# Expert layer of an eight-layer kernel: output product turned feature major, in float32r halves, with the token weights applied to the gated blocks

## The chip, the cores and the metric

The kernel runs on one core of one Trainium2 chip. The metric is the device time of one execution in microseconds, as the median of several runs. Profiles are of one execution; times in them are microseconds from the start of its span.

## The reference, cut to what matters

The program applies eight layers in a row to an activation of 2048 tokens with 128 features: attention and feed-forward layers in turn, each followed by a residual add and a layer norm. The change is in the fourth, a mixture of eight experts of which each token uses two:

```
gate_out = einsum('bsd,ed->bse', x, Wg)             # 8 logits per token
top_v, top_i = top_k(gate_out, 2)
probs = softmax(top_v)
for e in range(8):
    w_e = sum(probs * (top_i == e))                 # 0 for six of the eight
    h1 = einsum('bsd,hd->bsh', x, W1[e])            # 128 -> 256
    h2 = einsum('bsd,hd->bsh', x, W2[e])
    g = h1 * sigmoid(h1) * h2
    out = out + einsum('bsh,dh->bsd', g, W3[e]) * w_e
x = layernorm(x + out)
```

Every expert is computed for every token, and the weight (zero for most) is applied after.

## The kernel before, in words

The tokens lie in four batches of 512 (NB = 4), each as an SBUF tile X of 128 partitions by four chunks of 128 features. Eight stage classes run one after the other: Causal, F0, Rel, F1, Alibi, F2, A3, F3. F1 is the expert layer, lines 1939 to 2059.

The order of the work is written as Python generators that are stepped by hand: `K.step` (line 160) gives each generator of a list one turn, first the tails of the stage before; `K.tick` (line 148) gives one turn to the background list, which holds the set-up and the first batch of the *next* stage. A framework then places the instructions in each engine's queue by priority and by its own estimate of when operands are ready, and adds the semaphores. So each engine works strictly in order, but an instruction without open operands can stand far ahead of its place in the program. Tiles of one tag share a number of buffers (`bufs`); a new one waits until the oldest is free.

Float32 accuracy at float32r speed is had by halves: a value is split into a rounded part h and a rest l, and `mm3` (line 311) adds three products, wh·xh + wl·xh + wh·xl. `split_w` (line 290) loads a weight in chunks of 512 columns, casts h on VectorE and subtracts l on GpSimd.

In F1, `setup` (line 1949) loads and splits W1 and W2. `gate` (line 1969) works for one batch: it transposes X on TensorE (`xT`, line 317), copies X into the accumulator `acc` on GpSimd (line 1980), computes the logits (line 1984), ranks them on VectorE with a small GpSimd step (`rank`, line 1914), and leaves the weights `wt`, tokens on the partitions, in line 2000. `run` (line 2040) goes over batch b and expert e; each expert has two blocks of 128 hidden features (mm = 0, 1). `hidden` (line 2003) makes one block, hidden features on the partitions and 512 tokens along: six products of 512 columns into two PSUM banks, Silu on ScalarE (line 2012), and the product g of one bank with it on VectorE (line 2014). `out` (line 2017) follows one block later: for each of four chunks of tokens two float32 products with g as the stationary operand and W3 as the moving one (line 2025), which gives y with tokens on the partitions; then four scalar_tensor_tensor instructions on VectorE (line 2029) do acc = y · wt + acc. After the eighth expert the layer norm of `acc` writes X. The gate of the next batch is started at expert 2, and from the second batch on each block gives the next stage, Alibi, one background turn: its set-up, its first batch, and the maxima of scores (lines 695 and 697).

Of the kernel before, what the change touches and what calls it, by code (L numbers as in the profile page):

```python
# [7 lines left out]
F32 = mybir.dt.float32  # L8
F32R = mybir.dt.float32r
# [3 lines left out]
ALU = mybir.AluOpType  # L13
# [3 lines left out]
P = 128  # L17
NB = 4
T = 512
# [20 lines left out]
class K:  # L40
# [115 lines left out]
    def next(self):  # L156
        self.uid += 1
        return self.uid
# [131 lines left out]
    def split_w(self, pool, src, n, name, scales=(), tag=None, raw=("wraw", 1)):  # L290

        nc = self.nc
        h = pool.tile([P, n], F32R, name=name + "h", tag=(tag or name) + "h")
        l = pool.tile([P, n], F32R, name=name + "l", tag=(tag or name) + "l")

        def fill():
            for s in range(0, n, 512):
                e = min(n, s + 512)
                w = pool.tile([P, 512], F32, tag=raw[0], name=f"wraw{self.next()}", bufs=raw[1])
                self.late(nc.sync.dma_start(w[:, :e - s], src[:, s:e]))  # L300
                yield
                yield
                for a, b, f in scales:
                    if a <= s < b:
                        nc.vector.tensor_scalar(w[:, :e - s], w[:, :e - s], f, None, ALU.mult)
                nc.vector.tensor_copy(h[:, s:e], w[:, :e - s])
                nc.gpsimd.tensor_tensor(l[:, s:e], w[:, :e - s], h[:, s:e].bitcast(F32), ALU.subtract)
                yield
        return h, l, fill()

    def mm3(self, out, wh, wl, xh, xl):
        nc = self.nc
# [142 lines left out]
class Attn:  # L455
# [4 lines left out]
    nb, lead, lag, ahead = 3, 8, 5, 2  # L460
    span, keep = "last", True
# [167 lines left out]
class Causal(Attn):  # L629


    alibi, nm = False, "a0"

    def weights(self):
        k, d, pool = self.k, self.k.d, self.early
        h, l, fill = k.split_w(pool, d["a0_w"], 256, "a0wqk")
        next(fill)
        bqk = k.load(pool, d["a0_b"][0:256].rearrange("(a p) -> p a", p=P), [P, 2], "a0bqk")
        self.pads(0)
        wv = k.load(pool, d["a0_w"][:, 256:384], [P, P], "a0wv")  # L640
        bv = k.bcast(pool, d["a0_b"][256:384], P, "a0bv")
        wo = k.load(pool, d["a0_wo"], [P, P], "a0wo")
        bo = k.bcast(pool, d["a0_bo"], P, "a0bo")
        self.w = dict(qkh=h, qkl=l, v=wv, o=wo, bqk=bqk, bv=bv, bo=bo)
        yield from fill
# [57 lines left out]
    def rows_out(self, t, mx):  # L703
        k, nc, pool = self.k, self.nc, self.wk
        yield
        yield
        yield from k.turn(True)
        ps = k.bank("b")
        for c in range(4):
            k.tr(ps[:4, c * P:(c + 1) * P], mx[:, c, :])  # L710
        yield
        nm = pool.tile([4, T], F32R, tag="nm", name=f"nm{t}", bufs=2)
        nc.scalar.activation(nm, ps[:4, :], AF.Copy, scale=-1.0)
        self.mrow(t, nm)
        self.rows_at = t
        yield
# [82 lines left out]
class Alibi(Causal):  # L799
    MROW, alibi, nm = 30, True, "a2"  # L800
    nb, lead, pre, span = 4, 12, True, "first"
# [18 lines left out]
class Rel(Attn):  # L820
# [3 lines left out]
    R, MROW, NV, nm = 64, 48, 2, "a1"  # L824
    nb, lead, lag, ahead = 3, 6, 4, 3
# [302 lines left out]
class A3:  # L1128


    nm, span, keep, la = "a3", "last", True, 2
# [377 lines left out]
class F0:  # L1509


    nm, span, keep = "f0", "first", True
# [426 lines left out]
class F1:  # L1939


    nm, span, keep = "f1", None, True
    banks = dict(s=4, o=2, b=2)

    def __init__(self, k):
        self.k, self.nc = k, k.nc
        self.x, self.wt, self.acc = {}, {}, {}

    def setup(self):
        k, d, pool = self.k, self.k.d, self.early  # L1950
# [18 lines left out]
    def gate(self, b, X):  # L1969

        k, nc, w = self.k, self.nc, self.w
        u = k.next()
        pool = self.pool if b else self.early
        self.x[b] = yield from k.xT(pool, X, full=True, bufs=2 if b else 1)
        xf = self.x[b][2]
        if b == 0:
            acc = self.acc[b] = pool.tile([P, 4, P], F32, name="acc0")
        else:
            acc = self.acc[b] = k.sh.tile([P, 4, P], F32, tag="ot", name=f"acc{u}", bufs=2)
        nc.gpsimd.tensor_copy(acc, X)  # L1980
        yield from k.turn()
        ps = k.bank()
        for c in range(4):
            nc.tensor.matmul(ps[:, 8 * c:8 * c + 8], xf[:, c * P:(c + 1) * P], w["g"], start=True, stop=True)
        yield
        lg = pool.tile([P, 4, 8], F32, tag="lg", name=f"lg{u}", bufs=2)
        nc.vector.tensor_copy(lg, ps[:, :32].rearrange("p (c e) -> p c e", e=8))
        m = pool.tile([P, 4], F32, tag="m", name=f"m{u}", bufs=2)
        ex = pool.tile([P, 4, 8], F32, tag="ex", name=f"ex{u}", bufs=2)
        wt = self.early.tile([P, 4, 8], F32, tag="wt", name=f"wt{u}", bufs=2)  # L1990
        nc.vector.tensor_reduce(m, lg, AX.X, ALU.max)
        nc.vector.tensor_tensor(ex, lg, m[:, :, None].to_broadcast([P, 4, 8]), ALU.subtract)
        nc.scalar.activation(ex, ex, AF.Exp)
        yield
        rk = yield from rank(k, pool, lg, w["tri"], 8, 4, f"f1{u}")
        nc.vector.tensor_scalar(rk, rk, 1.5, None, ALU.is_lt)
        nc.vector.tensor_tensor(ex, ex, rk, ALU.mult)
        nc.vector.tensor_reduce(m, ex, AX.X, ALU.add)
        nc.vector.reciprocal(m, m)
        nc.vector.tensor_tensor(wt, ex, m[:, :, None].to_broadcast([P, 4, 8]), ALU.mult)  # L2000
        self.wt[b] = wt

    def hidden(self, b, e, mm):
        k, nc, w, pool = self.k, self.nc, self.w, self.pool
        xh, xl, _ = self.x[b]
        s = [k.bank("s") for _ in range(2)]
        for j in range(2):
            ws = slice(512 * e + 256 * j + P * mm, 512 * e + 256 * j + P * mm + P)
            k.mm3(s[j], w["1h"][:, ws], w["1l"][:, ws], xh, xl)
        u = k.next()  # L2010
        sl = pool.tile([P, T], F32, tag="sl", name=f"sl{u}", bufs=3)
        nc.scalar.activation(sl, s[0], AF.Silu)  # L2012
        g = pool.tile([P, T], F32, tag="g", name=f"g{u}", bufs=5)
        nc.vector.tensor_tensor(g, s[1], sl, ALU.mult)
        return g

    def out(self, b, e, gs, X):
        k, nc, w = self.k, self.nc, self.w
        acc = self.acc[b]
        while b not in self.wt:  # L2020
            yield
        y = k.bank("o")
        for c in range(4):
            for mm in range(2):
                nc.tensor.matmul(y[:, c * P:(c + 1) * P], gs[mm][:, c * P:(c + 1) * P], w["3"][:, 2 * e + mm, :],  # L2025
                                 start=(mm == 0), stop=(mm == 1))
        yield
        for c in range(4):
            nc.vector.scalar_tensor_tensor(acc[:, c, :], y[:, c * P:(c + 1) * P], self.wt[b][:, c, e:e + 1], acc[:, c, :],
                                           ALU.mult, ALU.add)  # L2030
        yield
        if e == 7:
            yield
            if b == NB - 1:
                k.layernorm(acc, X)
            else:
                yield from k.norm(acc, X)
            k.finish(self, b, X)

    def run(self, Xs):  # L2040
        k = self.k
        self.w["3"] = k.load(self.pool, k.d["f1_w3"], [P, 16, P], "f1w3")
        gs = []
        last = None
        for i in range(8 * NB + 1):
            b, e = divmod(i, 8)
            if e == 2 and b + 1 < NB:
                gs.append(self.gate(b + 1, Xs[b + 1]))
            g = []
            for mm in range(2):  # L2050
                if i < 8 * NB:
                    g.append(self.hidden(b, e, mm))
                if mm == 0 and last:
                    gs.insert(0, self.out(*last))
                k.step(gs)
                if b:
                    k.tick()
            last = (b, e, g, Xs[min(b, NB - 1)])
        k.leave(self, gs, 0)


class F2:
    nm, span, keep = "f2", None, False
# [116 lines left out]
class F3:  # L2180


    nm, span, keep = "f3", None, True
    lag, ahead, steps = 4, 7, 2
# [97 lines left out]
    def weigh(self, b, j, h):  # L2282
        k, nc, w = self.k, self.nc, self.w
        while b not in self.cT:
            k.step(self.gs)
        cb = k.bank("t")
        nc.tensor.matmul(cb, w["sel"][:, j, :], self.cT[b], start=True, stop=True)
        nc.vector.tensor_tensor(h, h, cb, ALU.mult)
# [119 lines left out]
```

## Time and profile before

| | us |
|---|---|
| median of 3 runs | 2244.88 (2244.24 to 2246.5) |
| the profiled execution, its time | 2239.62 |
| its span | 2237.9 |
| TensorE busy (matmuls) | 2025.4, 91% of the span |
| VectorE busy | 1664.1, 74% |
| ScalarE busy | 1333.5, 60% |
| GpSimd busy | 501.9, 22% |
| F1's output matmuls (line 2025), first to last start | 1053.9 to 1209.1 |
| F1's accumulation (line 2029), 128 instructions | 37.8 |

In the profile PE is TensorE's matmuls, PEld its weight loads, DVE is VectorE, ACT is ScalarE, POOL is GpSimd, SP the engine that issues most DMAs. An instruction is named by its line, its operation, what it writes and what it reads (`o<-f1w,g`), and its shapes. A row of a group gives its busy time, the mean duration in ns, and the idle time of the engine just before it with what ended that. Busy time of an engine is not work on the path: what a change in one stage is worth is read from that stage, and there from what ends last.

### The profile page before, as it was taken

The numbers are of one execution on the slowest core, as the hardware profiler recorded it, in microseconds if no ns is written. First come the engines' busy times: TensorE is split into PE (matmuls) and PEld (weight loads), VectorE is DVE, ScalarE is ACT, GpSimd is POOL, SyncE is SP. The second block draws the span as 40 slices with busy tenths as digits, with TensorE's granted clock in tenths as the row PEclk, the third lists the DMA queues.
The fourth block names the chain that finished last, engine by engine and source line by source line (L and its number), as shares of the span: only waits on it lengthen the run. The fifth ranks groups of instructions, "written<-read, shape, count | busy, mean of one in ns | idle before, by whom it ended". The sixth has DMA issues, their size and how long they took to land.

```text
span 2237.9 us, 43122 instructions
## 1 busy us (share of the span) xinstructions
PE 2025.4 (91%) x14400; PEld 1477.7 (66%) x14400; DVE 1664.1 (74%) x5592; ACT 1333.5 (60%) x2983; POOL 501.9 (22%) x706
## 2 busy tenths in 40 slices
PE   7999788888888999999999999998999999999897
PEld 4666566676665667676887665786666566666676
DVE  5778689888878677873777785544777877778787
ACT  3566787787734656665333666333777777767632
POOL 3222212111212532433000322531111111111220
PEclk9999999999978999999999999999999999999999
DMA  5321322021433454421021420604888878888400
GB/s 171 106 77 35 109 50 57 6 48 27 116 113 108 130 175 125 127 65 57 15 67 48 116 78 15 219 17 112 214 209 198 211 192 193 199 194 211 99 5 15
DMA packets 264918, 242.10 MB, mean 108 GB/s; under 512 B 106352, under 2 KB 190618, under 8 KB 263866
## 3 DMA queue, kind: packets, MB, share of 16 engines
q1 hardware_dynamic: 259146, 221.33, 37.2%
q0 software_dynamic: 5232, 17.50, 3.3%
q8 instruction: 115, 1.88, 0.3%
q14 instruction: 105, 0.86, 0.1%
q10 hardware_dynamic: 320, 0.52, 0.1%
HBM read 103.82 MB, written 74.32 MB: 80 GB/s over the span
## 4 chain that ended last, share of the span: by engine, by line
PE 59%; DVE 17%; ACT 10%; DMA 7%; issue 4%; POOL 2%; SPq 1%; ACTq 0%; POOLq 0%; DVEq 0%
PE t L219 5%; PE s L2129 4%; PE o L1393 3%; PE o L744 3%; PE s L695 3%; PE t L728 3%; PE o L1032 3%; PE b L313 3%; PE b L219 3%; PE o L2025 3%; DMA a3dpw<-p 2%; PE s L313 2%; PE b L315 2%; PE b L314 2%; PE s L315 2%
## 5 line engine op out<-in xcount | busy, mean ns | idle before, releaser
L985 DVE CUSTOM_DVE_ANT_0 junk<-w,a1mask 128x640 bf16<-128x640 f32 x256 | 203.1, 818 | 67.3 <-PE w L983 65.4
L219 PE MATMUL t<-ident,p 128*128 128x128 f32 x1280 | 201.9, 279 | 23.8 <-ACT p L1350 15.7
L772 ACT ACTIVATE Pt<-t 128x384 f32<-128x384 f32 (+1 forms) x384 | 179.5, 528 | 65.8 <-PE t L728 54.4
L219 PEld LDWEIGHTS t<-ident,p 128*128 128x128 f32 x1280 | 151.7, 142 | 81.0 <-ACT p L1350 39.0
L1363 ACT COPY PT<-t 128x512 f32<-128x512 f32 x256 | 149.9, 596 | 71.9 <-PE t L219 70.9
L1059 ACT ACTIVATE Pt<-t 128x512 f32<-128x512 f32 x256 | 149.1, 597 | 72.7 <-PE t L1058 44.5
L1350 ACT ACTIVATE p<-s,nb 128x512 f32<-128x512 f32 x256 | 178.6, 702 | 12.8 <-DVE nb L1349 8.4
L1349 DVE TENSOR_REDUCE nb<-s 128x1 f32<-128x512 f32 x256 | 175.0, 687 | 2.6
L1368 DVE CUSTOM_DVE_ANT_0 jk<-p,a3right 128x496 bf16<-128x496 f32 (+3 forms) x256 | 125.0, 488 | 29.2 <-ACT p L1350 17.8
L697 DVE CUSTOM_DVE_ANT_0 junk<-s,a0mask 128x128 bf16<-128x128 f32 (+3 forms) x256 | 114.2, 485 | 43.4 <-PE s L695 42.4
L697 DVE CUSTOM_DVE_ANT_0 junk<-s,a2mask 128x128 bf16<-128x128 f32 (+3 forms) x256 | 114.9, 484 | 28.3 <-PE s L695 27.9
L781 POOL TENSOR_SCALAR_AFFINE_SELECT Pt<-Pt 128x512 f32<-128x512 f32 x112 | 69.9, 636 | 249.0 <-ACT Pt L772 248.9
L1344 PE MATMUL s<-a3KT,a3QT 128*128 128x512 f32 x256 | 118.9, 465 | 7.3 <-DMA a3K<-L 4.1
L1347 DVE TENSOR_TENSOR s<-s,W 128x160 f32<-128x160 f32 (+1 forms) x256 | 81.1, 318 | 56.1 <-PE s L1345 55.2
L1393 PE MATMUL o<-PT,V 128*64 128x512 f32 x512 | 116.9, 599 | 0.5 <-ACT PT L1363 0.5
L1707 ACT ACTIVATE p<-sm,nb 128x128 f32<-128x128 f32 x256 | 100.6, 396 | 24.8 <-DVE nb L1705 24.3
L1345 PE MATMUL s<-a3K,a3Q 128*128 128x512 f32 x256 | 102.7, 401 | 0.1
L1705 DVE CUSTOM_DVE_ANT_0 sm<-s,band,rn 128x128 f32<-128x128 f32 x256 | 78.3, 344 | 26.5 <-PE s L1692 19.3
L1056 PE MATMUL t<-a1Q,a1K 128*128 128x512 f32 (+3 forms) x256 | 92.4, 366 | 6.2 <-ACT Pt L1059 3.6
L695 PE MATMUL s<-a0K,a0Q 128*128 128x256 f32 (+2 forms) x256 | 83.6, 387 | 14.0 <-DVE mx L697 6.8
L982 PE MATMUL w<-a1K,a1Q 128*128 128x256 f32 (+2 forms) x192 | 83.8, 437 | 9.3 <-DVE mx L985 8.3
L2012 ACT ACTIVATE sl<-s 128x512 f32<-128x512 f32 x64 | 38.0, 598 | 91.0 <-PE s L315 85.6
(494 smaller groups left out, 5812.7 us busy)
## 6 DMA issues: line engine op xcount, KB each, us to landing
W<-a3dsk SPq DMA_DIRECT2D x32, 640.0 KB
a1Q<-a1iq SPq DMA_DIRECT2D x32, 512.0 KB
a3dpw<-p SPq DMA_DIRECT2D x64, 160.0 KB
a3dpw<-p SPq DMA_DIRECT2D x64, 144.0 KB
a1K<-a1ik SPq DMA_DIRECT2D x64, 128.0 KB
a3Q<-a3dim SPq DMA_DIRECT2D x32, 256.0 KB
a3KT<-H POOLq DMA_DIRECT2D x64, 128.0 KB, 4.4
a3KT<-H SPq DMA_DIRECT2D x64, 128.0 KB
```

The lines of the kernel that those rows point to most:

```text
L219: return self.nc.tensor.matmul(out.bitcast(x.dtype), x, i[:n, :n], is_transpose=True, start=start, stop=stop)
L695: self.scored = nc.tensor.matmul(s[:, :nm], self.qof(0, t, i)[:, qc * P:(qc + 1) * P], Ks[:, i, :nm], start=True, stop=True).ins
L697: nc.vector.tensor_tensor_reduce(junk[:, :n], s[:, :n], k.mask[:, 512 - n:512], 1.0, NEG, ALU.add, ALU.max, mx[:, qc, i:i + 1])
L772: ready = nc.scalar.activation(Pt[:, i, z:], s[:, z:], AF.Exp, scale=sc).ins
L985: nc.vector.tensor_tensor_reduce(junk, s.rearrange("p a n -> p (a n)")[:, T - n:T + m], k.mask[:, T - n:T + m], 1.0, NEG, ALU.add, ALU.max ...
L1059: nc.scalar.activation(Pt[:, i, :T], s, AF.Exp, scale=sc)
L1344: nc.tensor.matmul(s, QT[:, e, qs], KT[:, e, :], start=True, stop=False)
L1349: nc.vector.tensor_reduce(nb, s, AX.X, ALU.min)
L1350: nc.scalar.activation(p[:, e, :], s, AF.Exp, bias=nb, scale=-1.0, accum_out=den[:, qc, 2 * un + e:2 * un + e + 1])
L1363: self.copied[t] = nc.scalar.copy(PT[e][:, :, qc * P:qc * P + P], tb.rearrange("p (c n) -> p c n", n=P)).ins
L1368: nc.vector.tensor_tensor_reduce(jk[:, :nn], p[:, e, x0:], w["right"][:, :nn], 1.0, 0.0, ALU.mult, ALU.add, at[:, e, qc, 31:32])
L1393: m = nc.tensor.matmul(o[64 * e:64 * e + 64, :], V[:, kc, h * 64:h * 64 + 64], PT[e][:, kc, :], start=(kc == 0), stop=False)
```

## The change

Only F1 and one helper are touched. W3 is now split into halves by `split_w` in the stage itself (its raw chunks use the buffers of the Silu outputs) and is the stationary operand; the gated block is the moving one. Each block of 128 hidden features gives three float32r products of 512 columns, and the 48 products of a batch accumulate in one PSUM bank, with output features on the partitions. The weights can then no longer be a scalar per partition. They are applied before: `gate` transposes them to 8 rows of 512 tokens, writes the rows to DRAM, and `weights` reads each row back, spread over all 128 partitions, as a 512-column tile `cb` (four buffers). `weigh` multiplies g by it on GpSimd, in place, copies the rounded half on ScalarE and subtracts the other on VectorE. `weigh` is called two blocks after `hidden`, `out` two after that. At the end of a batch the result is copied to SBUF, transposed back, and X is added on VectorE; the accumulator in SBUF, its copy of X and the 128 accumulations are gone. The cut diff:

```diff
+    def rows_out(self, rows, name):
+        n = rows.shape[0]
+        d = self.dr.tile([n, T], F32, tag=f"rows{n}", name=name, bufs=2)
+        self.nc.gpsimd.dma_start(d, rows)
+        return d
...
-    nm, span, keep = "f1", None, True
+    nm, span, keep, lag = "f1", None, True, 2
...
-        nc.gpsimd.tensor_copy(acc, X)
...
         nc.vector.tensor_tensor(wt, ex, m[:, :, None].to_broadcast([P, 4, 8]), ALU.mult)
-        self.wt[b] = wt
+        yield
+        yield from k.turn()
+        ps = k.bank()
+        for c in range(4):
+            k.tr(ps[:8, c * P:(c + 1) * P], wt[:, c, :])
+        yield
+        wr = pool.tile([8, T], F32, tag="wr", name=f"wr{u}", bufs=1)
+        nc.scalar.copy(wr, ps[:8, :])
+        self.rows[b] = k.rows_out(wr, f"f1rows{b}")
+        if b:
+            yield from self.weights(b)
+
+    def weights(self, b):
+        cb = self.wt[b] = []
+        for i in range(8):
+            cb.append(self.pool.tile([P, T], F32, tag="cb", name=f"cb{b}{i}", bufs=4))
+            self.nc.gpsimd.dma_start(cb[i], self.rows[b][i].partition_broadcast(P))
+            for _ in range(0 if b == 0 and i < 2 else 2):
+                yield
...
-        sl = pool.tile([P, T], F32, tag="sl", name=f"sl{u}", bufs=3)
+        sl = pool.tile([P, T], F32, tag="sl", name=f"sl{u}", bufs=2)
...
-        g = pool.tile([P, T], F32, tag="g", name=f"g{u}", bufs=5)
+        g = pool.tile([P, T], F32, tag="g", name=f"g{u}", bufs=self.lag + 1)
...
+    def weigh(self, b, e, g):
+        nc.gpsimd.tensor_tensor(g, g, self.wt[b][e], ALU.mult)
+        h, l = (pool.tile([P, T], F32R, tag="g" + x, name=f"g{x}{u}", bufs=3) for x in "hl")
+        nc.scalar.copy(h, g)
+        nc.vector.tensor_tensor(l, g, h.bitcast(F32), ALU.subtract)
+        return h, l
...
-        y = k.bank("o")
-        for c in range(4):
-            for mm in range(2):
-                nc.tensor.matmul(y[:, c * P:(c + 1) * P], gs[mm][:, c * P:(c + 1) * P], w["3"][:, 2 * e + mm, :],
-                                 start=(mm == 0), stop=(mm == 1))
-        yield
-        for c in range(4):
-            nc.vector.scalar_tensor_tensor(acc[:, c, :], y[:, c * P:(c + 1) * P], self.wt[b][:, c, e:e + 1], acc[:, c, :],
-                                           ALU.mult, ALU.add)
...
+        if i == 0:
+            self.acc[b] = k.bank("o")
+        y, (h, l) = self.acc[b], g
+        for n, (p, q) in enumerate(((w["3h"], h), (w["3l"], h), (w["3h"], l))):
+            nc.tensor.matmul(y, p[:, i * P:(i + 1) * P], q, start=(i == n == 0), stop=(i == 15 and n == 2))
+        if i < 15:
+            return
+        yield
+        yT = k.sh.tile([P, T], F32, tag="os", name=f"yT{b}", bufs=1)
+        nc.scalar.copy(yT, y)
+        yield
+        yield from k.turn()
+        ps = k.bank("b")
+        for c in range(4):
+            k.tr(ps[:, c * P:(c + 1) * P], yT[:, c * P:(c + 1) * P])
+        yield
+        r = k.sh.tile([P, 4, P], F32, tag="ot", name=f"r{b}", bufs=2)
+        nc.vector.tensor_tensor(r, ps.rearrange("p (c n) -> p c n", c=4), X, ALU.add)
...
-        self.w["3"] = k.load(self.pool, k.d["f1_w3"], [P, 16, P], "f1w3")
...
+        h, l, fill = k.split_w(self.pool, k.d["f1_w3"].rearrange("p a n -> p (a n)"), 2048, "f1w3", raw=("sl", 2))
+        self.w["3h"], self.w["3l"] = h, l
+        while 0 not in self.rows:
+            k.step(k.bg)
+        gs, q, r = [self.weights(0), fill], [], []
+        n, lag = 16 * NB, self.lag
+        for i in range(n + lag + 2):
+            b, j = divmod(i, 16)
+            if j == 2 and b + 1 < NB:
+                gs.append(self.gate(b + 1, Xs[b + 1]))
+            if i < n:
+                q.append(self.hidden(b, j // 2, j % 2))
+            if lag <= i < n + lag:
+                b, j = divmod(i - lag, 16)
+                while b not in self.wt or len(self.wt[b]) <= j // 2:
+                    k.step(gs)
+                r.append(self.weigh(b, j // 2, q[i - lag]))
+            if i >= lag + 2:
+                b, j = divmod(i - lag - 2, 16)
+                gs.insert(0, self.out(b, j, r[i - lag - 2], Xs[b]))
+            k.step(gs)
+            if i >= 16:
+                k.tick()
```

More of the change, by code (lines that the diff above doesn't have):

```diff
@@ L1946, in __init__ @@
         self.k, self.nc = k, k.nc
-        self.x, self.wt, self.acc = {}, {}, {}
+        self.x, self.wt, self.acc, self.rows = {}, {}, {}, {}
     def setup(self):
@@ L1975, in gate @@
         xf = self.x[b][2]
[L1976 to L1979, printed above, removed]
-        nc.gpsimd.tensor_copy(acc, X)
         yield from k.turn()
@@ L2010, in hidden @@
         u = k.next()
-        sl = pool.tile([P, T], F32, tag="sl", name=f"sl{u}", bufs=3)
+        sl = pool.tile([P, T], F32, tag="sl", name=f"sl{u}", bufs=2)
         nc.scalar.activation(sl, s[0], AF.Silu)
-        g = pool.tile([P, T], F32, tag="g", name=f"g{u}", bufs=5)
+        g = pool.tile([P, T], F32, tag="g", name=f"g{u}", bufs=self.lag + 1)
         nc.vector.tensor_tensor(g, s[1], sl, ALU.mult)
         return g
-    def out(self, b, e, gs, X):
-        k, nc, w = self.k, self.nc, self.w
-        acc = self.acc[b]
-        while b not in self.wt:
-            yield
-        y = k.bank("o")
+    def weigh(self, b, e, g):
+        k, nc, pool = self.k, self.nc, self.pool
+        u = k.next()
+        nc.gpsimd.tensor_tensor(g, g, self.wt[b][e], ALU.mult)
[3 more added lines that the diff above has]
+        return h, l
@@ new lines, in out @@
+    def out(self, b, i, g, X):
+        k, nc, w = self.k, self.nc, self.w
+        if i == 0:
[11 more added lines that the diff above has]
+        ps = k.bank("b")
@@ L2031, in out @@
+        nc.vector.tensor_tensor(r, ps.rearrange("p (c n) -> p c n", c=4), X, ALU.add)
         yield
[L2032 to L2038, printed above, removed]
+        if b == NB - 1:
+            k.layernorm(r, X)
+        else:
+            yield from k.norm(r, X)
+        k.finish(self, b, X)
     def run(self, Xs):
         k = self.k
-        self.w["3"] = k.load(self.pool, k.d["f1_w3"], [P, 16, P], "f1w3")
@@ L2043, in run @@
[L2043 to L2047, printed above, removed]
-                gs.append(self.gate(b + 1, Xs[b + 1]))
[L2049 to L2058, printed above, removed]
+        h, l, fill = k.split_w(self.pool, k.d["f1_w3"].rearrange("p a n -> p (a n)"), 2048, "f1w3", raw=("sl", 2))
```

## Prediction

> **What bounds the kernel now.** I read the page's chain first: TensorE ends last for 59% of the span and VectorE for 17%, and the old output matmuls (line 2025) are one of its lines, at 3%. That says where to look, not what a change there is worth, so I then cut the expert stage F1 into 20 us stretches. It fills 1050 to 1210 us.
>
> ```profile
> core 0: us, PE busy (x) PEld busy (x) DVE busy (x) ACT busy (x) POOL busy (x), PEclk, DMA share, GB/s
> 1070.00:1090.00 20.00, 20.00 (x121) 17.28 (x120) 13.29 (x42) 8.11 (x13) 1.29 (x4) 1.00 0.00 0
> 1150.00:1170.00 20.00, 20.00 (x122) 17.39 (x121) 15.49 (x51) 7.74 (x12) 1.85 (x5) 1.00 0.00 1
> 1190.00:1210.00 20.00, 20.00 (x131) 17.70 (x130) 12.28 (x39) 4.55 (x8) 0.00 (x0) 1.00 0.00 1
> sum 160.00, PE 158.18 PEld 138.84 DVE 118.01 ACT 52.98 POOL 15.23; mean PE 19.77 PEld 17.36 DVE 14.75 ACT 6.62 POOL 1.90
> ```
>
> TensorE has no gap at full clock; VectorE is busy 118.0 of 160 us, ScalarE 53.0, GpSimd 15.2. TensorE's order of work sets this stage. Third, the timeline of one expert (columns: start, duration, engine, line, operation), for the spacing of instructions, since a matmul's own duration overlaps its neighbours':
>
> ```profile
> 1130.40 0.40 PE L314 MATMUL s<-xTh,f1wl 128*128 128x512 f32 x1
> 1130.64 0.39 PE L315 MATMUL s<-xTl,f1wh 128*128 128x512 f32 x1
> 1130.87 1.95 PE L2025 MATMUL o<-f1w,g 128*128 128x128 f32 x16
> 1132.57 0.48 PE L313 MATMUL s<-xTh,f1wh 128*128 128x512 f32 x1
> 1132.85 1.13 DVE L2029 SCALAR_TENSOR_TENSOR acc<-o,wt,acc 128x128 f32<-128x128 f32 x4 [1.02 <-PE o L2025]
> 1132.89 0.40 PE L314 MATMUL s<-xTh,f1wl 128*128 128x512 f32 x1
> ```
>
> A 512-column float32r matmul starts 0.233 us after the one before. The eight float32 output matmuls of an expert run as 16 and take 1130.87 to 1132.66 (1132.89 less one spacing), 1.79 us; the chain has them at 1.78.
>
> **The change, part by part.**
>
> TensorE. Per expert the 1.79 us become 2 blocks x 3 products x 0.233 = 1.40 us, so 32 x 0.39 = 12.5 us go. Seven sets of four transposes come into the stage (weights of three batches; the result of four). A set in this stage takes about 0.45 us to the next matmul's start (1112.76 to 1113.11, plus that matmul's slow start), so 3.2 us. Net -9.3 us: **TensorE alone would need 150.7 us for the stretch.** The set for batch 0 lies in Rel, some 130 us ahead of its use (line 2000 runs at 915 us).
>
> ScalarE. 64 copies of the weighted block at 0.61 us (row of line 930) are 39 us, plus seven evacuations at 0.58: 53 + 43 = 96 us of 160, hidden under TensorE; a table reload is not to be expected, since copies already stand between the Silus today.
>
> VectorE. 32 groups of four scalar_tensor_tensors at 1.13 us go: -36.2. Added are 64 subtractions 128x512 at 0.64 (0.69 alone, 0.60 when the next follows at once): +41.0; four casts of W3 at 0.42 (line 306): +1.7; four adds of X at 0.69: +2.8. Sum 118.0 + 9.3 = 127.3 us. By the sum that still fits under 150.7.
>
> GpSimd. The two copies of X in the stretch go (-1.2). Added are 64 multiplications 128x512, which have a direct row elsewhere (line 1649), four subtractions for W3 of the same kind, and 32 broadcasts and 3 row writes, each an issue like line 1312's. That is 15.2 - 1.2 + 68 x 1.28 + 35 x 0.52 = 119 us. A broadcast also has to wait, on GpSimd's own queue, until its rows have landed in DRAM; landing takes 4.4 us (median of line 1312's issues), three times in the stretch: 132 us. Behind that wait stand the next multiplications, and for them ScalarE's copies. They have the two iterations of lag, some 4.5 us, as cover; a wait longer than that would stop TensorE.
>
> ```profile
> L1649 POOL TENSOR_TENSOR kr<-kr,tb 128x512 f32<-128x512 f32 x32 | 40.9, 1278 | 171.3 <-DVE kr L1641 136.6 <-DVE rs L351 8.4 <-DVE rs L344 6.5
> L1312 POOL DMA_DIRECT2D a3KT<-H x64 | 33.4, 524 | 173.1 <-ACT H L1307 153.6 <-ACT bd L1270 19.5
> L930 ACT CAST r0h<-t 128x512 fp32r<-128x512 f32 x4 | 2.5, 616 | 1.8 <-POOL t L925 1.8
> ```
>
> So each engine alone fits. **The cost is where GpSimd and VectorE meet.** Three pairs from the timelines of other stages:
>
> ```profile
> 1477.54 0.29 DVE L366 BATCH_NORM_STATS2 lnst<-r 128x6 f32<-128x128 f32 x1
> 1477.54 1.29 POOL L2092 TENSOR_TENSOR hhl<-h,hhh 128x512 fp32r<-128x512 f32 x1 [4.30 <-DVE hhh L2091]
> ...
> 1483.30 1.30 POOL L2092 TENSOR_TENSOR hhl<-h,hhh 128x512 fp32r<-128x512 f32 x1 [0.43 <-DVE rs L346]
> 1483.32 1.29 DVE L347 TENSOR_TENSOR rs<-rs,lnv 128x4 f32<-128x4 f32 x1
> ...
> 349.48 1.28 POOL L1649 TENSOR_TENSOR kr<-kr,tb 128x512 f32<-128x512 f32 x1 [3.98 <-DVE kr L1641]
> 349.92 1.46 DVE L1639 TENSOR_TENSOR tb<-ta,tab 128x256 f32<-128x256 f32 x2
> ```
>
> In the first, a VectorE instruction with one SBUF input runs beside GpSimd's at its usual 0.29. In the second, a tiny one with two SBUF inputs (median 0.155) takes 1.29 and ends with GpSimd's. In the third, two large ones with two SBUF inputs (about 0.76 for the pair) take 1.46. The stage today has next to none of this, because GpSimd is nearly idle and both 128x512 operands of line 2014 are not in SBUF. The new subtraction reads g and h, both in SBUF; the new multiplication runs 64 times. The two exclude each other.
>
> What a subtraction waits: from nothing (it always slips in ahead) to 1.28 us (always behind a whole multiplication). I take the middle in two ways. Multiplications fill 82 of 160 us, so a random arrival waits 0.51 x 0.64 = 0.33 us. Laid out by hand at TensorE's pace (block product in VectorE, then multiplication, copy, subtraction), the waits alternate between 0 and about 0.8, mean 0.41. So 64 x 0.33 to 0.41 = 21 to 26 us. The small two-input instructions of four layer norms and three gates (some 15 each, 105 in all) come in runs, of which I let a third wait 0.33: 11 us. VectorE then needs 127.3 + 24 + 11 = 162 us, more than TensorE's 150.7, and in an order that waits for ScalarE and TensorE as well; 4 us for that gives **166 us in place of 160, +6 us**. The outer ends are 150.7 (no wait) and 127.3 + 64 x 1.28 = 209 us.
>
> A rule that speaks against the new DMAs on GpSimd: line 1312's 64 issues, the nearest row, span only 0.516 to 0.551 us, so the sum above takes 0.52. The Trainium skill, "SBUF — State Buffer", section "SBUF: two separate sides", says that a DMA issued by GpSimd starves while VectorE runs a two-port copy, some 620 ns alone becoming 3100. An estimate from that page, for the four W3 casts alone, would be 4 x 2.5 = 10 us more on GpSimd; the trace of before shows no such case, and the sum goes by the row.
>
> Ends of the stage. At its start W3 (1 MB, one DMA now) comes in four chunks through the buffers of Silu; the first output block is now due two iterations later, after about 1056 us, and chunk and broadcast, issued near 1048.5, should land by 1053: nothing, or 2 us if a broadcast is late. At its end the result passes one copy, four transposes and an add before the norm, some 3 us later; Alibi's first matmuls cover batch 3, and batch 0's, four to five steps later, push about one unit of Alibi's maxima (0.6 us) past the stage. I count +1 and -1 (four copies of X and the DVE stalls behind Alibi's memsets today) as nothing.
>
> **Rivals.** (1) TensorE keeps setting the pace: if the subtractions mostly run right after the block product, before the multiplication has started, they wait little; spare VectorE time is 150.7 - 127.3 = 23 us, that is 0.36 us per subtraction. For: it stands right behind the block product in VectorE's queue, while the multiplication must first be told that the product is done. Against: its own copy from ScalarE must be done by then. It gives -9 us, 2235 to 2236 (by the median). This is the case on the other side; it decides when the mean wait is under 0.2 us, with 64 x 0.2 + 11 = 24. (2) GpSimd becomes the bound: its 132 us plus 64 waits behind subtractions of up to 0.6 (38 us) are 170, and bunched in the batches that also hold Alibi's four memsets (1.8 us each) and the W3 split; 175 to 190 us, +15 to +30. For: a queue that also waits for DMAs. Against: batch 3 has none of that. (3) The gains and waits cancel, -4 to +2.
>
> **How the numbers follow.** The sum is made against the profiled execution, 2239.6 us (span 2237.9). Runs shown have a median of 2244.9, 5.3 above, so I add 5.3: 2239.6 + 6 + 5.3 = 2251 us. Chances: forecast (+2 to +14) 0.42; TensorE bound (-4 to -11) 0.27; GpSimd bound 0.18; cancelled 0.13. A measurement of this kernel can tell about 0.2%, 4.5 us. Of the forecast's 0.42 about 0.09 lies under that, so faster 0.27, same 0.22, slower 0.51. The range 2235 to 2273 reaches from TensorE's bound to nearly the end of GpSimd's case. Cases of both signs hold much; the forecast's own range is 2247 to 2259.
>
> **What would show it.** Right: in 1050 to 1210, subtractions with a mean above 0.9 us ending together with multiplications, TensorE idle for VectorE or waiting for the halves at the output matmuls, GpSimd near 80% busy. TensorE's step is right if an expert's six output matmuls take 1.40. Rival 1 shows in subtractions of 0.69 and TensorE at 20.00 in every stretch. Rival 2 shows in ScalarE waiting for GpSimd, and GpSimd for row DMAs. Wrong in kind: a different order of instructions after the stage, or Alibi starting late.

## The result and the profile after

The changed kernel takes 2271.55 us (median of 5 runs, 2268.40 to 2277.44) against 2244.88 before: ratio 1.0126, interval 1.0104 to 1.0148. It is slower, as forecast, but by 26.7 us and not by 6. The profiled execution took 2273.53 us (span 2271.7).

The stage is now read from F1's first Silu to its last: 155.5 us before (1050.5 to 1206.0), 184.2 after (1056.2 to 1240.4). These 28.7 us are most of the 33.8 by which the two profiled spans differ; the first Silu itself comes 5.7 us later. The share of the chain that ended last has moved from TensorE to VectorE and to waits (page of the kernel after, shares of the span; before, TensorE had 59% and VectorE 17%):

```profile
PE 53%; DVE 20%; ACT 10%; DMA 6%; issue 6%; POOL 3%; SPq 1%; ACTq 0%; POOLq 0%; DVEq 0%
```

The stretches of the kernel after (columns as in the table of the prediction; three parts of the stage, then the whole):

```profile
core 0: us, PE busy (x) PEld busy (x) DVE busy (x) ACT busy (x) POOL busy (x), PEclk, DMA share, GB/s
1062.00:1086.00 24.00, 15.38 (x62) 11.07 (x61) 23.68 (x51) 10.29 (x17) 19.82 (x16) 0.94 0.49 164
1110.00:1134.00 24.00, 23.33 (x107) 18.18 (x105) 20.17 (x48) 14.76 (x26) 17.96 (x18) 1.00 0.23 73
1160.00:1185.00 25.00, 19.89 (x74) 15.74 (x72) 16.94 (x53) 11.14 (x18) 10.92 (x13) 0.80 0.45 133
1056.00:1246.00 190.00, 160.52 (x676) 119.77 (x675) 160.83 (x326) 90.31 (x156) 130.22 (x121) 0.96 0.28 85
```

TensorE was idle 1.8 of 160 us before (busy 158.18 in the sum of the prediction's table) and is now idle for 29.5 of 190. The last row holds the surprise of this case: VectorE is busy 160.8 us (forecast 162), GpSimd 130.2 (forecast 132). The loads came out as worked out, and yet the stage takes 190 us and not 166. The groups that answer to the rows of the prediction (kernel after, 1056 to 1246):

```profile
L2042 POOL TENSOR_TENSOR g<-g,cb 128x512 f32<-128x512 f32 x64 | 90.7, 1424 | 48.2 <-DVE g L2035 34.1 <-DMA cb<-f1rows 2.5 <-DVE rs L358 2.0
L2045 DVE TENSOR_TENSOR gl<-g,gh 128x512 fp32r<-128x512 f32 x64 | 68.3, 1067 | 20.2 <-ACT gh L2044 19.9
L356 DVE TENSOR_SCALAR rs<-rs 128x4 f32<-128x4 f32 x4 | 4.8, 1191 | 0.0
```

GpSimd's multiplication takes 1424 ns (1278 where it was looked up), the subtraction 1067 (0.64 to 0.69 us by itself), and an instruction on 128x4 elements 1191 ns. The same instruction before (lines of the kernel before, 1049 to 1210):

```profile
L349 DVE TENSOR_SCALAR rs<-rs 128x4 f32<-128x4 f32 x4 | 0.7, 164 | 0.0
```

The other rows of the stretches say why the loads do not give the time: in the first stretch VectorE is full and TensorE loses a third, in the second TensorE is nearly full and VectorE has room, in the third both wait and the clock is down. A sum over the whole stage lets the room of one stretch pay for another, and the kernel can't.

What TensorE waited for, and the chain behind it (waits of the kernel after, 1056 to 1246; total us, times, longest):

```profile
ACT gh L2044 <- POOL g L2042: 66.7, 48, 3.3
POOL g L2042 <- DVE g L2035: 34.1, 23, 5.0
DVE gl L2045 <- ACT gh L2044: 19.9, 20, 2.3
PE s L320 <- DVE g L2035: 15.2, 16, 3.4
PE s L702 <- issue: 4.8, 1, 4.8
PE b L219 <- DVE wt L2002: 4.6, 2, 2.6
PE s L320 <- ACT sl L2033: 2.9, 2, 1.8
```

Three things are seen. TensorE waits 15.2 us for VectorE's block product (line 2035), which frees its PSUM bank. VectorE itself waits 19.9 us for ScalarE's half, and that for GpSimd's multiplication. And TensorE stops once for 4.8 us at line 702, Alibi's first score.

How a block product comes late (timeline of the kernel after):

```profile
1066.21 3.16 DVE L377 TENSOR_SCALAR lnv<-lnmv 128x4 f32<-128x4 f32 x1
1066.29 1.31 POOL L2042 TENSOR_TENSOR g<-g,cb 128x512 f32<-128x512 f32 x1
...
1067.51 1.82 POOL L537 MEMSET a2K<- 128x2048 f32 x1
...
1069.48 0.69 DVE L2035 TENSOR_TENSOR g<-s,sl 128x512 f32<-128x512 f32 x1
...
1070.23 0.50 PE L320 MATMUL s<-xTh,f1wh 128*128 128x512 f32 x1 [1.85 <-DVE g L2035]
```

A VectorE instruction on 128x4 elements, 0.17 us in the run with the multiplication on VectorE, lasts 3.16 us: it ends with the memset, the *second* GpSimd instruction after it was due. (The trace has the subtraction behind it start at 1067.54, between the two GpSimd instructions, and end with it, so how much of the second wait is whose is open here; a cast in the run with halves, below, shows the same alone.) The block product stands behind it in VectorE's queue, and TensorE waits 1.85 us for that. The Trainium skill, "SBUF — State Buffer", section "Who interferes with whom", says that where the two engines contend, the one that issues first has the shared ports for the whole instruction and the other is blocked. The blocking agrees; a wait of 3.16 us, over two GpSimd instructions end to end, is more than that sentence would give.

The stop at line 702 (timeline of the kernel after; SPq are DMA issues):

```profile
1158.74 1.58 SPq L546 DMA_DIRECT2D a2ik<-qh  x1
...
1163.26 0.39 PE L2055 MATMUL o<-gh,f1w3h 128*128 128x512 f32 x1
...
1163.49 0.39 PE L2055 MATMUL o<-gh,f1w3l 128*128 128x512 f32 x1
...
1163.72 0.40 PE L2055 MATMUL o<-gl,f1w3h 128*128 128x512 f32 x1
...
1165.16 7.86 SPq L563 DMA_DIRECT2D a2K<-a2ik  x16
1169.41 0.55 PE L702 MATMUL s<-a2K,a2Q 128*128 128x256 f32 x1 [4.84 <-issue]
...
1172.32 0.63 PE L2055 MATMUL o<-gh,f1w3h 128*128 128x512 f32 x1
...
1172.75 0.63 PE L2055 MATMUL o<-gh,f1w3l 128*128 128x512 f32 x1
```

Alibi's operands go to DRAM and come back; the sixteen transfers of their load are issued from 1165.16 on and TensorE, which reached the first score at about 1164.6, starts it at 1169.4. The profile names no releaser for this wait ("issue"); that it is the late load is tested below. The output products are spaced 0.23 us before the stop, as forecast (1.40 for six), and 0.43 after it, at a granted clock of 0.74 from 1160 to 1180.

### The profile page after: what moved, and what is told of

Same layout as the page of the kernel before. It is cut to its first block, busy times and chain, and to the rows that moved or that the text cites. A ratio compares the mean times of both kernels' runs of the same rounds, so it can differ in the third digit from the quotient of the medians.

```text
span 2271.7 us, 42792 instructions
## 1 busy us (share of the span) xinstructions
PE 2032.2 (89%) x14112; PEld 1458.8 (64%) x14112; DVE 1709.5 (75%) x5536; ACT 1372.8 (60%) x3055; POOL 618.7 (27%) x806
## 3 DMA queue, kind: packets, MB, share of 16 engines
q8 instruction: 113, 1.85, 0.3%
## 4 chain that ended last, share of the span: by engine, by line
PE 53%; DVE 20%; ACT 10%; DMA 6%; issue 6%; POOL 3%; SPq 1%; ACTq 0%; POOLq 0%; DVEq 0%
PE t L219 5%; PE s L2171 4%; PE o L1400 3%; PE o L751 3%; PE s L702 3%; PE t L735 3%; PE o L1039 3%; PE b L219 3%; PE b L320 2%; PE t L1063 2%; PE b L322 2%; PE b L321 2%; POOL g L2042 2%; PE w L989 1%; PE s L1352 1%
## 5 line engine op out<-in xcount | busy, mean ns | idle before, releaser
L219 PE MATMUL t<-ident,p 128*128 128x128 f32 x1280 | 200.8, 278 | 22.2 <-ACT p L1357 13.5
L1066 ACT ACTIVATE Pt<-t 128x512 f32<-128x512 f32 x256 | 148.8, 597 | 74.7 <-PE t L1065 44.2
L2042 POOL TENSOR_TENSOR g<-g,cb 128x512 f32<-128x512 f32 x64 | 90.7, 1424 | 48.2 <-DVE g L2035 34.1
L1393 POOL CAST a<-at 128x256 fp32r<-128x256 f32 x32 | 13.1, 408 | 304.4 <-DMA at<-a3dpw 150.6
```

Of the source, the lines that this page charges most:

```text
L219: return self.nc.tensor.matmul(out.bitcast(x.dtype), x, i[:n, :n], is_transpose=True, start=start, stop=stop)
L1066: nc.scalar.activation(Pt[:, i, :T], s, AF.Exp, scale=sc)
L2042: nc.gpsimd.tensor_tensor(g, g, self.wt[b][e], ALU.mult)
```

## The experiments

Theory A: VectorE and GpSimd exclude each other where VectorE's instruction has two SBUF inputs or is a copy, cast or scale within SBUF, block products wait in line behind, and TensorE for them. B: the stage's start and Alibi's late data. C: the chain through GpSimd, ScalarE and VectorE is too long. D: VectorE's own load. All edits are to the changed kernel; ratios are to the kernel before on the same chip. The runs were made on several chips, so differences between two runs are taken from the ratios, times 2247 us; by the intervals they are known to some 4 to 9 us.

| run | median us | ratio | interval | first to last Silu, us |
|---|---|---|---|---|
| before (two profiles) | | 1 | | 155.5, 155.6 |
| changed kernel | 2271.55 | 1.0126 | 1.0104 to 1.0148 | 184.2 |
| no multiplication | 2242.69 | 0.9972 | 0.9960 to 0.9984 | 150.3 |
| Alibi later | 2268.71 | 1.0104 | 1.0084 to 1.0125 | 178.7 |
| multiplication on VectorE | 2261.68 | 1.0066 | 1.0051 to 1.0082 | 165.5 |
| memsets on ScalarE | 2276.46 | 1.0133 | 1.0116 to 1.0150 | 180.9 |
| multiplication beside | 2267.96 | 1.0096 | 1.0074 to 1.0117 | 177.2 |
| three iterations behind | 2264.31 | 1.0079 | 1.0064 to 1.0094 | 174.3 |
| upper half from PSUM | 2263.75 | 1.0080 | 1.0048 to 1.0112 | 170.7 |
| three edits at once | 2255.96 | 1.0036 | 1.0022 to 1.0050 | 162.5 |
| multiplication in halves | 2274.64 | 1.0127 | 1.0095 to 1.0160 | 188.9 |
| on VectorE, later and further behind | 2254.01 | 1.0037 | 1.0023 to 1.0051 | 156.6 |

**No multiplication.**

```diff
-        nc.gpsimd.tensor_tensor(g, g, self.wt[b][e], ALU.mult)
```

> The GpSimd multiplication by the token weights is left out (line 2042), so the blocks go into the output product unweighted; its broadcasts, copies, subtractions and products stay. Theory A (VectorE and GpSimd exclude each other on instructions with two SBUF inputs, block products stand behind those waits in VectorE's queue, TensorE waits for them): subtractions near 0.7 us, norms at their durations of before, TensorE's waits for the block product (15 us or more) nearly gone; 20 to 30 us less than the changed kernel, 2241 to 2252. Theory B (the late data of Alibi's first scores, the 4.8 us stop at line 702 with the clock at 0.74 to 0.80 after it, and the stage's start): at most 5 us less, 2266 to 2272. Theory C (GpSimd's own length of chain, broadcasts included): like A in time, but norms and casts of VectorE stay long.

Measured 0.9972: some 35 us less than the changed kernel ((1.0126 - 0.9972) x 2247; 29 by the medians), as theory A gave or more, and under the kernel before. VectorE and the whole stage in that run:

```profile
1056.00:1212.00 156.00, 150.13 (x681) 120.74 (x681) 128.36 (x329) 94.18 (x156) 39.61 (x57) 0.98 0.34 104
```

```profile
L2044 DVE TENSOR_TENSOR gl<-g,gh 128x512 fp32r<-128x512 f32 x64 | 49.4, 774 | 8.2 <-ACT gh L2043 5.3 <-PE b L219 1.8 <-PE b L321 0.4
L377 DVE TENSOR_SCALAR lnv<-lnmv 128x4 f32<-128x4 f32 x4 | 5.8, 1454 | 0.0
```

Without GpSimd's multiplication the changed stage is what the forecast took for TensorE alone: 150.1 us busy of 156 (forecast 150.7), VectorE 128.4 (forecast 127.3 without waits). The start and the broadcasts were still there, so they are not the main cause. The stop at line 702 was 1.5 us in that run; what it is worth by itself is read from the run with Alibi later. Line 377 still waits (1454 ns), for the memsets that remain. The run doesn't tell A from C, since both go with the multiplication.

**Multiplication beside**, which separates them.

```diff
-            cb.append(self.pool.tile([P, T], F32, tag="cb", name=f"cb{b}{i}", bufs=4))
+            cb.append(self.pool.tile([P, T], F32, tag="cb", name=f"cb{b}{i}", bufs=3))
...
-        nc.gpsimd.tensor_tensor(g, g, self.wt[b][e], ALU.mult)
+        j = pool.tile([P, T], F32, tag="side", name=f"side{u}", bufs=1)
+        nc.gpsimd.tensor_tensor(j, g, self.wt[b][e], ALU.mult)
```

> As in the run without the multiplication, the blocks go unweighted into the output product; but GpSimd still makes all 64 multiplications, into a tile that nobody reads (for its room the buffers of the broadcast weights are three in place of four). So GpSimd is as busy beside VectorE as in the changed kernel, and nothing waits for its results. Theory A (exclusion on two SBUF inputs): subtractions and norms wait as in the changed kernel (36 us in all over the stage, its subtractions 1.07 us each), TensorE waits for block products: 2260 to 2272. Theory C (the chain product, GpSimd, ScalarE, VectorE is too long for its two iterations of lag): as without the multiplication, 2240 to 2249. In between, 2250 to 2259, both have a share.

Measured 1.0096. Nobody waits for GpSimd's result, and 28 of the 35 us are there nonetheless ((1.0096 - 0.9972) x 2247). VectorE's groups in that run, GpSimd's, and the stage:

```profile
L2046 DVE TENSOR_TENSOR gl<-g,gh 128x512 fp32r<-128x512 f32 x64 | 77.8, 1217 | 1.7 <-ACT gh L2045 0.8 <-PE b L219 0.5
L377 DVE TENSOR_SCALAR lnv<-lnmv 128x4 f32<-128x4 f32 x4 | 6.8, 1704 | 0.0
```

```profile
1052.00:1235.00 183.00, 160.26 (x681) 122.99 (x680) 169.80 (x327) 92.92 (x156) 129.64 (x121) 0.94 0.30 89
```

The subtractions take 1217 ns, more than in the changed kernel, VectorE is busy 169.8 of 183 us. That is theory A with the chain taken away. The remaining 7 us are at most the chain's (theory C), and part of them may be the stop at line 702, 2.6 us here; the intervals of this run and of the changed kernel overlap, so that share is not settled by this run.

**Multiplication on VectorE.**

```diff
-        nc.gpsimd.tensor_tensor(g, g, self.wt[b][e], ALU.mult)
+        nc.vector.tensor_tensor(g, g, self.wt[b][e], ALU.mult)
```

> The multiplication by the token weights is issued on VectorE in place of GpSimd. VectorE gets 64 x 0.66 = 42 us more of its own work in the stage and GpSimd loses 82. Theory A: the waits for GpSimd go, VectorE needs 127 + 42 = 169 us plus little, 160 + 10 for the stage, some 5 to 10 for the start and Alibi: 2257 to 2266, faster than the changed kernel in spite of the 42 us. If VectorE's plain load is what the stage lacks (theory D): slower than the changed kernel, 2285 or more.

Measured 1.0066, 13 us less than the changed kernel by the ratios (10 by the medians) though VectorE does 64 instructions more. The groups of that run show what each costs when GpSimd is quiet:

```profile
L2045 DVE TENSOR_TENSOR gl<-g,gh 128x512 fp32r<-128x512 f32 x62 | 45.1, 743 | 5.1 <-ACT gh L2044 4.9
L2042 DVE TENSOR_TENSOR g<-g,cb 128x512 f32<-128x512 f32 x64 | 44.1, 701 | 0.3 <-DMA cb<-f1rows 0.3
```

The multiplications take 44 us of VectorE's time. Against the run without them they cost 21 us of the kernel's time ((1.0066 - 0.9972) x 2247), where on GpSimd they cost 35. Theory D is out.

**Upper half from PSUM.**

```diff
-    banks = dict(s=4, o=2, b=2)
+    banks = dict(s=4, o=1, b=2, h=1)
...
         nc.scalar.copy(h, g)
-        nc.vector.tensor_tensor(l, g, h.bitcast(F32), ALU.subtract)
+        hp = k.bank("h")
+        nc.scalar.copy(hp, h.bitcast(F32))
+        nc.vector.tensor_tensor(l, g, hp, ALU.subtract)
```

> The upper half is copied once more by ScalarE, into a PSUM bank (64 copies of 0.6 us; the bank comes from the output accumulators, one in place of two), and the subtraction reads that one, so it has only one input in SBUF. GpSimd's multiplication and the chain stay, the chain 0.6 us longer. Theory A: subtractions fall from 1.07 to about 0.7 us, their 22 us of waits go, only the norms, gates and casts still wait (14 us): 12 to 22 us less than the changed kernel, 2250 to 2260. Theory C: no gain, 2270 or more.

```profile
L2047 DVE TENSOR_TENSOR gl<-g,h 128x512 fp32r<-128x512 f32 x64 | 46.0, 718 | 16.1 <-ACT h L2046 7.2 <-issue 6.8 <-PE s L322 0.9
L382 DVE TENSOR_SCALAR X<-r,lnmv,rs 128x128 f32<-128x128 f32 x16 | 11.8, 904 | 0.0
```

With one SBUF input instead of two, and GpSimd just as busy beside it, the subtraction takes 718 ns instead of 1067; the norms still wait (904 ns). Some 10 us less by the ratios (8 by the medians), barely clear of noise and short of the 12 to 22 expected: this run also has the stop at line 702 (6.8 us here) and TensorE waiting 4.7 us for the lower half, with a chain that is a copy longer. That the subtraction no longer waits is shown; theory C's "no gain" is thereby unlikely, its length of chain is not.

**Three iterations behind**, the test of the chain.

```diff
-    nm, span, keep, lag = "f1", None, True, 2
+    nm, span, keep, lag = "f1", None, True, 3
...
-            cb.append(self.pool.tile([P, T], F32, tag="cb", name=f"cb{b}{i}", bufs=4))
+            cb.append(self.pool.tile([P, T], F32, tag="cb", name=f"cb{b}{i}", bufs=3))
```

> The weighting comes three iterations behind the block product in place of two (for the room of one more block, the broadcast weights have three buffers in place of four). Theory C: one iteration more, 2.3 us, for a chain that waits for GpSimd up to 3.3 us: 8 to 20 us less than the changed kernel, 2252 to 2264. Theory A: the same GpSimd work beside the same VectorE work, within 4 us, 2267 to 2275.

Measured 1.0079, some 10 us less by the ratios (7 by the medians), where theory A alone gave at most 4. VectorE's wait for the upper half falls from 19.9 to 2.6 us; its busy time does not fall (stage and wait of that run):

```profile
1054.00:1234.00 180.00, 156.63 (x673) 118.70 (x672) 167.30 (x324) 92.98 (x155) 128.59 (x120) 0.97 0.31 90
```

```profile
DVE gl L2045 <- ACT gh L2044: 2.6, 5, 1.1
```

So the chain has a share of its own on top of the exclusion, at most these 10 us: the stop at line 702 is gone in this run too (longest wait there 1.2 us, clock 1.00 from 1160 to 1180 in place of 0.74), and the next run prices that at up to 5 us. How the 10 us divide is open.

**Alibi later.**

```diff
             yield from self.load(0)
+            for _ in range(4):
+                yield
             for i in range(16 + self.lead):
```

> Four idle steps are put between Alibi's first load of its operands and its first scores, nothing else. Theory B: TensorE no longer stops at line 702 for data (4.8 us), the stretch of 25 us at clock 0.80 behind it goes back to 1.00 (5 us); two units of maxima of 0.6 us move out: 7 to 10 us less than the changed kernel, 2262 to 2265. Theory A alone: TensorE then waits for VectorE in the same place, no more than 3 us less, 2268 to 2272.

The stop at line 702 is gone, the clock from 1160 to 1180 is 1.00 and no longer 0.74, and the stage is 5.5 us shorter (the stretch in the changed kernel, then in this run):

```profile
1160.00:1180.00 20.00, 15.16 (x55) 12.21 (x54) 12.03 (x26) 7.14 (x13) 8.82 (x8) 0.74 0.52 154
```

```profile
1160.00:1180.00 20.00, 16.68 (x81) 12.76 (x80) 18.29 (x50) 11.91 (x21) 12.06 (x15) 1.00 0.60 179
```

The medians differ by 2.8 us, and the intervals overlap: that the stop goes is shown, its price of 3 to 5 us (medians, ratios) is less than expected and not resolved. So theory B is out as the main cause. TensorE's wait for the block product rises from 15.2 to 18.2 us, so part of the stop had probably only covered it.

**Memsets on ScalarE.**

```diff
-            if nm == "a1":
+            if nm in ("a1", "a2"):
                 nc.scalar.activation(...)
```

> The four memsets of Alibi's K (1.8 us each on GpSimd, line 537) are made on ScalarE instead (a copy with scale 0); all else is as in the changed kernel. Theory A with its size in the bunching: the norm and cast instructions of VectorE that waited 2.1 to 3.2 us behind a multiplication and a memset wait for one instruction at most, 4 to 7 us less, 2264 to 2268. If the memsets only use time that VectorE had left: within 2 us, 2269 to 2273.

No gain: 1.0133, the same as the changed kernel within the noise, as the second expectation had it. The norm instruction of line 377 falls from 912 to 163 ns, but the subtractions rise from 1067 to 1134 and ScalarE now spends 7.6 us on the copies, in the queue in which Silu and the upper half stand. Taking out the longest single waits gave nothing; the waits came back on other instructions.

**Multiplication in halves.**

```diff
-        nc.gpsimd.tensor_tensor(g, g, self.wt[b][e], ALU.mult)
+        for s in (slice(0, 256), slice(256, 512)):
+            nc.gpsimd.tensor_tensor(g[:, s], g[:, s], self.wt[b][e][:, s], ALU.mult)
```

> GpSimd multiplies the block in two instructions of 256 columns (128 in place of 64, about 0.65 to 0.73 us each by the row of line 307's 128x256), nothing else is changed. If a VectorE instruction that comes late waits for the end of one GpSimd instruction (theory A in its simplest form): the mean wait halves, 15 us less VectorE time, 8 to 15 us less than the changed kernel, 2257 to 2264. If GpSimd has the next instruction ready and takes the pair of engines again first: the waits stay, 2268 to 2275 or a little more for 64 more instructions.

Nothing: 1.0127, and the subtractions take 1071 ns in place of 1067. The timeline of that run shows why (x2: both halves):

```profile
1064.11 1.44 POOL L2043 TENSOR_TENSOR g<-g,cb 128x256 f32<-128x256 f32 x2
1064.81 2.77 DVE L306 CAST f1w3h<-wraw 128x512 fp32r<-128x512 f32 x1
1065.48 1.81 POOL L537 MEMSET a2K<- 128x2048 f32 x1
```

The cast, 0.42 us of work, is held through the second half and the whole memset that follows. When GpSimd has its next instruction ready, it goes on and VectorE stays out; shorter instructions did not help here.

**The kernel before again**, unchanged.

> The kernel before, unchanged, for a second profile. In its first profile the expert stage's first Silu stands at 1050.5 us, in those of the changed kernel and of four experiments at 1054.8 to 1056.5. If the 4 to 6 us belong to the change (the added set of transposes, the row write and a new order in Rel's end): again 1050 to 1051.5. If they belong to the single execution: 1053 to 1056.

1051.7, near the first reading, but in the eleven profiles with the change it lies between 1048.1 and 1056.5. From Rel's first score to F1's first Silu it takes 397.2 and 398.8 us before, and a median of 401.1 with the change (395.3 to 401.5). Some 3 us at the end of Rel are likely the change's; they are not shown.

**Three edits at once**: upper half from PSUM, three iterations behind, Alibi later.

> Three earlier edits at once on the changed kernel: the upper half copied once more into PSUM for the subtraction (7.8 us less by itself), the weighting three iterations behind (7.3 less), Alibi's first scores four steps later (2.8 less; these three are the medians of those runs against 2271.55). If the three costs (VectorE's waits, the chain through GpSimd, the late data) are separate and the sum holds: 18 us less, 2253, that is 5 above the kernel before. If TensorE then sets the pace again: 8 to 10 us less than that, 2243 to 2245, as without the multiplication. If they are one and the same slack, counted three times: 2261 to 2264, no better than the best single one.

1.0036, about 16 us less than the changed kernel by the medians (20 by the ratios). Summed one by one the three give 18 by the medians and 26 by the ratios, so they are not one slack counted three times. Wholly separate they are not either, since the third iteration and the later Alibi both take away the stop at line 702. It is still slower than before, with VectorE's norms waiting and TensorE losing time in the first 20 us of the stage (13.5 of 20 busy from 1060 to 1080).

**On VectorE, later and further behind**: the multiplication on VectorE with the other two edits.

> The multiplication on VectorE, together with the weighting three iterations behind and Alibi's first scores four steps later; the subtraction reads two SBUF inputs as in the changed kernel. GpSimd hardly works, so VectorE has no waits for it, but its own work is 157 us in the run with the multiplication there (172 us of stage, 15 idle). If those 15 us were the chain and the late data: 8 to 12 us less than that run, 2250 to 2254, within 4 of the run that read the upper half from PSUM. If VectorE's load alone keeps the stage at 165: 2258 to 2262. A time under the kernel before needs a stage under 156 us, less than VectorE's own work: neither theory gives it.

1.0037. The stage now takes 156.6 us, about as before, with TensorE busy 153.0 and VectorE 148.8 of 160. The remaining 8 us lie outside the stage: likely some 3 in front of it, the scores moved out behind it, and a part that single profiles do not resolve. No version with the weights applied beat the kernel before. The only faster one left the weighting out; there the exchange of products brought 6 us.

## Why the prediction was right in sign and wrong in size

- **TensorE, -9.3 us: right where it is let go.** Six products take 1.40 us, and without the multiplication it is busy 150.1 us against 150.7. In the changed kernel it is 160.5: the granted clock is 0.96 over the stage, 1.00 before, and by an estimate from these two, 0.04 x 190 = 7.6 us of that is slower clock. The forecast counted TensorE at full clock even where it was to wait.
- **VectorE's load and waits, 162 us: right in total, in part by luck.** 160.8 measured. The subtractions wait 1067 - 743 = 324 ns each, by the run with a quiet GpSimd, 21 us (forecast 21 to 26). Half of them hardly wait (median 763 ns), some very long (up to 2303). The small instructions of lines 382, 356, 377, 306 and 352 alone take 15 us more than in that run (forecast 11 for all). The forecast let only small instructions with two SBUF inputs wait; these are scales and casts of one tile.
- **GpSimd's 132 us: right by luck.** 130.2 are busy. The forecast's sum had 13 us of waiting for row writes, which is not busy time; the changed kernel shows no such wait, and a row write landed in 1.8 us (median) and not in 4.4. In its place the multiplications take 146 ns more each (9 us in all).
- **The step that failed: "and in an order that waits for ScalarE and TensorE as well; 4 us for that".** Measured are 190 - 160.8 = 29 us in which VectorE is idle, and that makes the stage 190 us and not 166. Two things are behind it. The chain product, GpSimd, ScalarE, VectorE does not fit in its two iterations of lag: VectorE is idle 19.9 us for the upper half, and the third iteration takes that wait away, for a gain of at most 10 us. And VectorE's 36 us of waits do not come evenly: from 1062 to 1086 they fill it to 23.7 of 24 us, block products stand behind them, TensorE stops, and what VectorE has free later does not give that time back; this second part is read from the stretches and not tested by a run of its own. So the stage is a sum of stretches with different limits, not the largest of three sums.
- **The cover of "some 4.5 us" for GpSimd's broadcasts** was enough: GpSimd's multiplications waited 2.5 us for them in all.
- **"Alibi's first matmuls", counted as +1 and -1:** a wait that the forecast named only as "wrong in kind". Batch 0's result comes some steps later, Alibi's operands land 4.8 us after TensorE asks for them, and the clock falls. Its price is 3 to 5 us, not clear of noise.
- **Rivals.** TensorE setting the pace would have needed a mean wait under 0.2 us; it was 0.32. Of GpSimd as the bound (+15 to +30) the size fits and the mechanism only half: GpSimd is busy 130 of 190 us and is no bound, but ScalarE waits 66.7 us for it.

## What to carry to other kernels

Moving work to an idle GpSimd is not free for VectorE: price each VectorE instruction with two SBUF inputs, and each small one of a norm, as if it stood in GpSimd's queue, then ask who stands behind it. Add the stage up in stretches, since a wait in the stretch where VectorE is full stops TensorE and free time later doesn't give it back. When a subtraction must run beside GpSimd, one operand in PSUM frees it (718 in place of 1067 ns); when a chain passes through three engines, an iteration of lag more is a cheap test.

## What the hardware showed that was not expected

- VectorE stayed shut out through two GpSimd instructions in a row (2.77 us for a cast of 0.42; the 3.16 us for 128x4 elements are the less clear case), and cutting GpSimd's instructions in half left the mean wait where it was (1071 and 1067 ns).
- After 4.84 us without a matmul the next ones were spaced 0.43 us in place of 0.23; with the stop removed, the clock of those 20 us was 1.00 instead of 0.74. The Trainium skill, "TensorE: Matmul & The Clock Gate", section "Part 1: The HAM clock gate", gives half the clock after an idle window of about 3.4 us; 0.23 to 0.43, 1.8 times, is near that. Earlier in the stage a wait of 3.37 us left the spacing at 0.23, and one of 3.20 us, 5.6 us later, was followed by 0.43 (clock 0.64 from 1082 to 1086), so the length of the last wait alone does not tell (timeline of the kernel after):

```profile
1078.04 0.50 PE L320 MATMUL s<-xTh,f1wh 128*128 128x512 f32 x1 [3.37 <-DVE g L2035]
...
1078.62 0.40 PE L322 MATMUL s<-xTl,f1wh 128*128 128x512 f32 x1
1078.85 0.39 PE L2055 MATMUL o<-gh,f1w3h 128*128 128x512 f32 x1
...
1083.60 0.80 PE L320 MATMUL s<-xTh,f1wh 128*128 128x512 f32 x1 [3.20 <-DVE g L2035]
...
1084.62 0.63 PE L322 MATMUL s<-xTl,f1wh 128*128 128x512 f32 x1
1085.05 0.63 PE L2055 MATMUL o<-gh,f1w3h 128*128 128x512 f32 x1
```

- GpSimd's DMA issues beside a busy VectorE took 536 to 621 ns in the changed kernel, 536 to 613 without the multiplication; issues longer by 2.5 us, which the prediction weighed, did not occur in these two runs.
